# One limit and one power for the lengths of q and k, and the last group's attention mask applied after the exponential

## The chip, the cores and the metric

The kernel runs on one core of a Trainium2 chip. The time is what the device takes for one launch, in microseconds; of the kernel before there are three runs and one profiled execution.

The engines are called as in the profile: PE is TensorE (matrix products and transposes), PEld its loading of weights, DVE is VectorE, ACT is ScalarE, POOL is GpSimd, and SP is the engine whose queue issues most of the DMA transfers. L994 is line 994 of the kernel before.

## The reference

The input is 32 sequences of 256 tokens with 256 features in float32. First a recurrent block works on all of them: a projection to 512 channels and a gate, a causal convolution of four taps, a layer norm, a state of 16 x 512 that is updated and clipped token by token, and a projection back to 256. Then two transformer layers follow, and the input is added at the end. The change concerns the attention of these layers:

```python
h = shift_token(x)
q, k, v = jnp.split(h @ wqkv, 3, axis=-1)      # 8 heads of 64
q = l2norm(q) * qs                             # t / clip(norm(t), 1e-12), per token and head
k = l2norm(k) * ksc
q, k = rotary_xpos(q, k)
sim = jnp.einsum('bhwid,bhwjd->bhwij', bq * 8, bk)
mask = (i < j) | (i > j + WINDOW) | (j == -1)  # window of 128, causal
sim = jnp.where(mask, -finfo.max, sim)
out = jnp.einsum('bhwij,bhwjd->bhwid', softmax(sim), bv)
x = x + out @ wo
```

A query sees the keys of its own window of 128 tokens that are not later than itself, and those keys of the window before that lie at most 128 tokens back. With 256 tokens there are two windows. After the attention comes a feed-forward network with a gelu gate of width 682.

## The kernel before

**Stages.** The 32 sequences form four groups of 8. The recurrence (the scan) runs over a whole group at once, with 256 steps per group, and each step is one DVE instruction (L703) on a state of 128 x 512. Its results go to DRAM and are loaded again as the residual tiles for the layers. The layers then work on one sequence at a time. The order is group, layer, sequence: 4 x 2 x 8 = 64 passes, called sequences below. While the layers work on one group, the scan of the next groups is mixed in between; for the last group no scan is left, and its 16 passes run by themselves.

**Order.** The program is written as a pipeline by hand. Each of the 64 passes has 8 slots (`ST = 8`), and `stage(n, i, ...)` puts a piece of work into slot i of pass n. `attend` (L1393) places the attention's pieces: the scores in slots 2, 3 and 5, the row sums and the weighted values in slot 7, the division and the output projection in the slots of the next pass, and in the same slots the projections of the next pass's v (slots 0 and 3), q and k (slots 1 and 4), with the transposes of q and k in slots 6 (first window) and 8 (second window). `feed` (L1411) places the feed-forward network two passes later. A planner then orders the instructions of each engine, by the order in which they were written and by its own estimate of when their inputs are ready; `keep_in_program_order` pins an instruction behind what its engine was given before. [...]

**q and k.** `project_qkv` (L957) multiplies 128 tokens by the weights into a PSUM bank. `rotated` (L971) then does, for q and again for k: the squares on ACT (L975), the two products with the rotary tables on DVE (L978, L983), their sum on POOL (L986), the sum of squares per head on DVE (L988), a lower limit for it on DVE (L992), the power -1/2 on POOL (L994), and the multiplication of the rotated tile by it on POOL (L995). `turn` (L998) transposes the tile on PE and copies it by ACT.

**Scores and mask.** `scores` (L1153) makes scores with the keys as rows and the queries as columns, for one window of keys and a number of head pairs. It fills two PSUM banks of 128 x 512. In each bank the first matmul multiplies an identity by the mask, in bfloat16, and so writes 0 or -32768 (L1161); the matmuls of q and k add to it (L1168). The exponential on ACT (L1177) turns masked places into 0. A pass has three such calls, with two banks each: keys of window 1 (slot 2, `kw` = 1, four head pairs by 128 queries), and keys of window 0 for two head pairs by 256 queries at a time (slots 3 and 5). `sums` (L1181) and `values` (L1198) read the tiles pT from SBUF. There are 6 buffers for pT, one pass's worth, and 8 PSUM banks for everything.

A branch at the start takes an exact form of the program (`exact`, with a row maximum) where the scales of q and k are large; with these inputs it is not taken.

Of the kernel before, what the change touches and what calls it, by code (L numbers as in the profile page):

```python
# [19 lines left out]
P = 128  # L20
# [53 lines left out]
def kernel(  # L74
# [88 lines left out]
    for j in range(NJ):  # L163
# [23 lines left out]
        fill=MASKED_LOW, base=0, pattern=[[-1, W]], channel_multiplier=1,  # L187
    )

    head_cols = const.tile([P, 2, 32], FP, tag="head_cols", name="head_cols")  # L190
# [28 lines left out]
    def program(ctx, exact):  # L219
# [750 lines left out]

        def rotated(l, ps, w, a):  # L971


            sq = ap_.tile([P, DI], FP, tag="swp", name="sq", bufs=3)
            nc.scalar.activation(sq, ps, AF.Square)  # L975
            rot = ap_.tile([P, HEADS, DH], FP, tag="rot", name="rot", bufs=4)
            ph = ps.rearrange("p (h d) -> p h d", h=HEADS)
            nc.vector.tensor_mul(rot, ph, bc(rc_sb[:, l, w, a], 1, HEADS))  # L978
            swp = ap_.tile([P, HEADS, DH], FP, tag="swp", name="swp", bufs=3)
            hd = DH // 2  # L980
            for i in range(2):
                o, s = slice(i * hd, (i + 1) * hd), slice((1 - i) * hd, (2 - i) * hd)
                nc.vector.tensor_mul(  # L983
                    swp[:, :, o], ph[:, :, s], bc(rs_sb[:, l, w, a, o], 1, HEADS)
                )
            nc.gpsimd.tensor_add(rot, rot, swp)  # L986
            ss = aw.tile([P, HEADS], FP, tag="ss", name="ss")
            nc.vector.tensor_reduce(  # L988
                ss, sq.rearrange("p (h d) -> p h d", h=HEADS), AX.X, ALU.add
            )  # L990

            nc.vector.tensor_scalar_max(ss, ss, 1e-24)  # L992
            rn = aw.tile([P, HEADS], FP, tag="rn", name="rn")
            nc.gpsimd.tensor_tensor(rn, ss, neg_half, ALU.pow)  # L994
            nc.gpsimd.tensor_mul(rot, rot, bc(rn, 2, DH))  # L995
            return rot

# [37 lines left out]
        def attention(l):  # L1035

            for b in range(GB):

                qTs, kTs, vs = [], [], []
                for w in range(NW):  # L1040
                    for a in (2, 0, 1):
                        ps = project_qkv(b, w, a)
                        if a == 2:
# [3 lines left out]
                            continue  # L1047
                        rot = rotated(l, ps, w, a)
                        dst = ap_.tile(
# [77 lines left out]
        class Attention:  # L1127

            def __init__(self, l):
                self.l = l
                self.qkv, self.rot, self.p, self.o = {}, {}, {}, {}

            def project(self, b, w, a):
# [6 lines left out]
                if a == 2:  # L1142
                    nc.scalar.copy(self.qkv[b][2][:, w], ps)
                else:
                    self.rot[b, w, a] = rotated(self.l, ps, w, a)

# [6 lines left out]
            def scores(self, b, kw, i0, n):  # L1153
# [5 lines left out]
                for r in range(2):  # L1159
                    sc = ps_w.tile([P, n, nq], FP, tag="w", name="sc")  # L1160
                    nc.tensor.matmul(  # L1161
                        sc, ident_b, bc(mask_t[:, 0:nq], 1, n), start=True, stop=False
                    )
                    banks.append(sc)
                for i in range(n):
                    for r in range(2):
# [4 lines left out]
                            qT[rows, i0 + i, kw * W :],  # L1171
                            start=False,
                            stop=(i == n - 1),
                        )
                for r in range(2):
                    p = aw.tile([P, n, nq], FP, tag="pT", name="pT", bufs=6)
                    nc.scalar.activation(p, banks[r], AF.Exp)  # L1177
                    for i in range(n):
                        self.p[b, kw, i0 + i, r] = p[:, i, :]

            def sums(self, b):  # L1181
# [211 lines left out]
        def attend(n, at, b, nxt):  # L1393
# [3 lines left out]
            stage(n, 2, at.scores, b, 1, 0, HEADS // 2)  # L1397
            stage(n, 5, at.scores, b, 0, 2, 2)
            stage(n, 7, at.sums, b)
            stage(n, 7, at.values, b)  # L1400
# [33 lines left out]

        ats = [Attention(l) for _, l, _ in seqs]

# [157 lines left out]
```

## Time and profile before

| | |
|---|---|
| median of three runs | 3718.45 us |
| lowest and highest run | 3712.51 and 3718.55 us |
| profiled execution, its own time | 3716.42 us |
| its span, first to last instruction | 3714.5 us |
| TensorE clock granted, mean | 0.989 |
| attention's first instruction on POOL (L986) | 506.8 us |
| last step of the scan (L703) starts | 2876.3 us |
| mask matmuls (L1161) | 384 |
| limits (L992) and powers (L994) of q and k | 256 each |

The page gives busy times of the engines over the span, a strip of 40 slices, the chain of work that ended last, and groups of instructions by line. A group shows count, busy time in us, mean duration in ns of one, and after the second bar the time that the engine stood idle before instructions of this group, with the instruction that ended most of it. Matmuls overlap, so the duration of one is longer than the step to the next; the step is read from the chain, whose pieces follow each other in time.

### The profile page before, as it was taken

Reading aid. Unit: us, or ns where it says so; the run is one execution under the profiler, and the core shown is the slowest. Engines: PE = TensorE matmul, PEld = TensorE weight load, DVE = VectorE, ACT = ScalarE, POOL = GpSimd, SP = SyncE. Lnnn points to the kernel's source line nnn. Section 1 sums busy time; section 2 is a strip of 40 time slices with the busy share of each in tenths; the row PEclk is TensorE's granted clock in tenths of the full one; section 3 lists DMA queues with packets and bytes.
Section 4 is the critical chain, followed back from the end, with each engine's and each line's share of the span. In section 5 each row is a group of like instructions: output and inputs, shape, how many; then the busy total and the mean of one; then the engine's idle time right before and its main releaser. Section 6 shows DMA issues by size and latency. Waiting matters only on the chain.

```text
span 3714.5 us, 56989 instructions
## 1 busy us (share of the span) xinstructions
PE 3594.4 (97%) x19900; PEld 2240.4 (60%) x19900; DVE 2671.9 (72%) x5113; ACT 2161.5 (58%) x3689; POOL 1775.9 (48%) x1712
## 2 busy tenths in 40 slices
PE   7999889999999999999999999999999999999999
PEld 4444335666566566666666666666666666666666
DVE  5888889888787877887778777887776444444443
ACT  3666656666666666666666666666666444444442
POOL 4433366445455555554556555554444444433441
PEclk9999999999999999999999999999999999999999
DMA  7777655445454545445454546445453211011101
GB/s 205 203 198 203 185 164 149 130 110 135 121 140 122 150 129 150 125 112 133 110 138 124 140 138 148 126 108 137 106 135 98 60 35 50 12 35 33 30 27 36
DMA packets 469212, 435.79 MB, mean 117 GB/s; under 512 B 228835, under 2 KB 308532, under 8 KB 468788
## 3 DMA queue, kind: packets, MB, share of 16 engines
q1 hardware_dynamic: 384466, 420.05, 41.7%
q10 hardware_dynamic: 84450, 12.01, 2.1%
q8 instruction: 160, 2.62, 0.3%
q14 instruction: 136, 1.11, 0.1%
HBM read 383.70 MB, written 46.66 MB: 116 GB/s over the span
## 4 chain that ended last, share of the span: by engine, by line
PE 66%; DVE 15%; DMA 6%; POOL 5%; ACT 4%; issue 3%; SPq 0%; ACTq 0%; DVEq 0%; POOLq 0%
PE ps_qkv L962 13%; PE pa L1309 13%; PE po_f L1337 8%; DVE h L703 6%; PE y L715 5%; PE ps_wo L1012 4%; DMA xrep<-xnd 4%; PE sc L1168 4%; PE ov L1206 3%; PE ps_out L793 2%; PE ps_in L395 2%; PE tr_qk L1001 2%; ACT xrep L693 2%; DVE acc L485 2%; PE rs L1187 2%
## 5 line engine op out<-in xcount | busy, mean ns | idle before, releaser
L703 DVE CUSTOM_DVE_ANT_0 h<-h,xrep,lim 128x512 f32<-128x512 f32 x1024 | 950.2, 928 | 235.4 <-ACT xrep L693 200.8
L693 ACT ACTIVATE xrep<-xrep,beta 128x512 f32<-128x512 f32 x960 | 673.7, 719 | 342.5 <-DMA xrep<-xnd 252.5
L962 PE MATMUL ps_qkv<-qkv,res 128*128 128x512 f32 x1536 | 724.4, 607 | 18.4 <-DVE ag L1325 8.1
L1309 PE MATMUL pa<-hT,w 128*128 128x256 f32 (+1 forms) x3072 | 688.8, 386 | 1.4 <-ACT hT L1288 0.7
L1309 PEld LDWEIGHTS pa<-hT,w 128*128 128x128 f32 (+1 forms) x3072 | 492.7, 178 | 186.1 <-issue 77.4
L986 POOL TENSOR_TENSOR rot<-rot,swp 128x512 f32<-128x512 f32 x256 | 335.2, 1309 | 505.4 <-DVE swp L983 399.0
L962 PEld LDWEIGHTS ps_qkv<-qkv,res 128*128 128x128 f32 x1536 | 277.8, 191 | 327.9 <-issue 251.1
L994 POOL TENSOR_TENSOR rn<-ss,neg_half 128x8 f32<-128x8 f32 x256 | 459.2, 1794 | 15.2 <-DVE ss L992 5.2
L1325 DVE SCALAR_TENSOR_TENSOR ag<-pa,b_sb,ag 128x256 f32<-128x256 f32 (+1 forms) x448 | 213.4, 476 | 259.8 <-ACT ag L1317 257.3
L1337 PE MATMUL po_f<-ag,w 128*128 128x256 f32 (+1 forms) x1536 | 386.9, 393 | 11.6 <-DVE ag L1325 7.7
L715 PE MATMUL y<-h,ly 128*32 128x512 f32 x2048 | 356.5, 611 | 14.0 <-DVE h L703 13.1
L1337 PEld LDWEIGHTS po_f<-ag,w 128*128 128x128 f32 (+1 forms) x1536 | 272.7, 189 | 119.0 <-issue 52.0
L1262 POOL TENSOR_TENSOR rstd<-ve,neg_half 128x2 f32<-128x2 f32 x64 | 46.3, 723 | 622.3 <-DVE ve L1260 604.0
L995 POOL TENSOR_TENSOR rot<-rot,rn 128x512 f32<-128x512 f32 x256 | 292.4, 1142 | 20.1
L975 ACT ACTIVATE sq<-ps_qkv 128x512 f32<-128x512 f32 x256 | 151.9, 595 | 227.7 <-PE ps_qkv L962 175.7
L1317 ACT ACTIVATE ag<-pa,b_sb 128x256 f32<-128x256 f32 x320 | 150.2, 469 | 202.4 <-PE pa L1309 201.3
L978 DVE TENSOR_TENSOR rot<-ps_qkv,rc_sb 128x512 f32<-128x512 f32 x256 | 174.8, 683 | 82.9 <-ACT sq L975 82.2
L485 DVE SCALAR_TENSOR_TENSOR acc<-xr,wc_sb,acc 128x256 f32<-128x256 f32 x384 | 194.1, 529 | 53.7 <-POOL acc L474 53.2
L1012 PE MATMUL ps_wo<-oT,wo 128*128 128x256 f32 x1024 | 231.8, 379 | 0.2 <-ACT ag L1317 0.2
L1177 ACT ACTIVATE pT<-sc 128x512 f32<-128x512 f32 x384 | 208.5, 596 | 23.9 <-PE sc L1168 22.4
L1168 PE MATMUL sc<-qT,kT 64*128 64x128 f32 (+1 forms) x2048 | 222.0, 346 | 0.0
L1012 PEld LDWEIGHTS ps_wo<-oT,wo 128*128 128x128 f32 x1024 | 194.2, 190 | 28.3 <-ACT ag L1317 1.2
(150 smaller groups left out, 5437.0 us busy)
## 6 DMA issues: line engine op xcount, KB each, us to landing
xrep<-xnd SPq DMA_DIRECT2D x960, 256.0 KB
rb<-inv SPq DMA_DIRECT2D x128, 256.0 KB
xnd<-xn SPq DMA_DIRECT2D x64, 256.0 KB
qkv<-in_wqkv_dram SPq DMA_DIRECT2D x24, 512.0 KB
ahead<-xs_a SPq DMA_DIRECT2D x48, 256.0 KB
xp<-ahead SPq DMA_DIRECT2D x48, 256.0 KB
xd<-xnd SPq DMA_DIRECT2D x192, 64.0 KB
w<-in_w_dram SPq DMA_DIRECT2D x80, 128.0 KB
```

The costliest lines, as they stand in the source:

```text
L485: nc.vector.scalar_tensor_tensor(acc, xr[:, :, k : k + CH], wc_sb[:, ch, k : k + 1], acc, ALU.mult, ALU.add,)
L693: scaled = nc.scalar.activation(bx, ck[c].pop(("bx", t), bx), AF.Copy, scale=ck[c]["beta"][:, t : t + 1])
L703: nc.vector._custom_dve(TENSOR_ADD_SAT, out=h_new, in0=state["h"], in1=bx, s0=ck[c]["lim"][:, 0, t : t + 1], s1=ck[c]["lim"][:, 1, t : t + 1],
L715: nc.tensor.matmul(ck[c]["y", hb][32 * q : 32 * q + 32, :], ly[hb % 2][:, 32 * t : 32 * t + 32], ck[c].pop(("h", hb * TB + t)), start=(i = ...
L962: nc.tensor.matmul(ps, res[b][:, k, t0 : t0 + W], wt["qkv", a][:, k], start=(k == 0), stop=(k == KM - 1),)
L986: nc.gpsimd.tensor_add(rot, rot, swp)
L994: nc.gpsimd.tensor_tensor(rn, ss, neg_half, ALU.pow)
L995: nc.gpsimd.tensor_mul(rot, rot, bc(rn, 2, DH))
L1012: nc.tensor.matmul(po[:, d], wt["wo", 0][:, c, d * P : (d + 1) * P], oT[:, c, :], start=(c == 0), stop=(c == NC_ - 1),)
L1168: nc.tensor.matmul(banks[r][:, i, :], kT[rows, i0 + i, kw * W : (kw + 1) * W], qT[rows, i0 + i, kw * W :], start=False, stop=(i == n - 1),)
L1309: nc.tensor.matmul(pg if x else pa, wt["w1", m][:, k, x], self.h[:, k], start=(k == 0), stop=(k == KM - 1),)
L1337: nc.tensor.matmul(self.po[:, d], wt["w2", 0][r0 : r0 + n, m, d * P : (d + 1) * P], self.ag[m][r0 : r0 + n], start=(m == 0), stop=(m == le ...
```

## The change

The change has two parts.

First, the lengths of q and k of one window are kept in one tile of 128 x 2 x 8. `rotated` gets its half of it and ends with the sum of squares; a new function `normed` applies the limit and the power once to both halves (16 columns) and then multiplies the two rotated tiles. It is called after k, in the same slot in which k's rotation was before.

Second, the passes of the last group (`apart`) write no mask into PSUM. Every matmul of q and k there starts and stops its own accumulation. After the exponential, a new function `mask` multiplies the tile pT by a mask of ones and zeros in bfloat16, made once at the start on POOL. For the keys of window 1 this is done on POOL, in slot 3; for those of window 0 on DVE, in slots 4 and 6. Each of these multiplications is pinned behind what its engine was given before. The other three groups keep the mask matmul.

```diff
--- before.py
+++ after.py
@@ -186,6 +186,9 @@
         out=mask_t[:, W : 2 * W], in_=mask_t[:, W : 2 * W], compare_op=ALU.is_ge,
         fill=MASKED_LOW, base=0, pattern=[[-1, W]], channel_multiplier=1,
     )
+
+    mask_1 = const.tile([P, 2 * W], BF, tag="mask_1", name="mask_1")
+    nc.gpsimd.tensor_scalar(mask_1, mask_t, -1.0, None, ALU.is_ge)
 
     head_cols = const.tile([P, 2, 32], FP, tag="head_cols", name="head_cols")
     nc.gpsimd.memset(head_cols, 0.0)
@@ -968,7 +971,7 @@
                 )
             return ps
 
-        def rotated(l, ps, w, a):
+        def rotated(l, ps, w, a, ss):
 
 
             sq = ap_.tile([P, DI], FP, tag="swp", name="sq", bufs=3)
@@ -984,16 +987,22 @@
                     swp[:, :, o], ph[:, :, s], bc(rs_sb[:, l, w, a, o], 1, HEADS)
                 )
             nc.gpsimd.tensor_add(rot, rot, swp)
-            ss = aw.tile([P, HEADS], FP, tag="ss", name="ss")
             nc.vector.tensor_reduce(
                 ss, sq.rearrange("p (h d) -> p h d", h=HEADS), AX.X, ALU.add
             )
+            return rot
+
+        def lengths():
+            return aw.tile([P, 2, HEADS], FP, tag="ss", name="ss")
+
+        def normed(rots, ss):
+
 
             nc.vector.tensor_scalar_max(ss, ss, 1e-24)
-            rn = aw.tile([P, HEADS], FP, tag="rn", name="rn")
-            nc.gpsimd.tensor_tensor(rn, ss, neg_half, ALU.pow)
-            nc.gpsimd.tensor_mul(rot, rot, bc(rn, 2, DH))
-            return rot
+            rn = aw.tile([P, 2, HEADS], FP, tag="rn", name="rn")
+            nc.gpsimd.tensor_tensor(rn, ss, bc(neg_half, 1, 2), ALU.pow)
+            for a, rot in enumerate(rots):
+                nc.gpsimd.tensor_mul(rot, rot, bc(rn[:, a], 2, DH))
 
         def turn(rot, dst):
             tr = ps_w.tile([P, HEADS // 2, W], FP, tag="w", name="tr_qk")
@@ -1045,7 +1054,11 @@
                             nc.scalar.copy(v_sb, ps)
                             vs.append(v_sb)
                             continue
-                        rot = rotated(l, ps, w, a)
+                        if a == 0:
+                            rots, ss = [], lengths()
+                        rots.append(rotated(l, ps, w, a, ss[:, a]))
+                    normed(rots, ss)
+                    for a, rot in enumerate(rots):
                         dst = ap_.tile(
                             [P, HEADS // 2, W], FP, tag="kT1" if a else "qT1",
                             name="kT" if a else "qT", bufs=3 if a else 2,
@@ -1128,9 +1141,11 @@
 
 
 
-            def __init__(self, l):
+            def __init__(self, g, l):
                 self.l = l
-                self.qkv, self.rot, self.p, self.o = {}, {}, {}, {}
+
+                self.apart = g == NG - 1
+                self.qkv, self.rot, self.p, self.ps, self.o = {}, {}, {}, {}, {}
 
             def project(self, b, w, a):
                 if w == 0 and a == 2:
@@ -1142,7 +1157,11 @@
                 if a == 2:
                     nc.scalar.copy(self.qkv[b][2][:, w], ps)
                 else:
-                    self.rot[b, w, a] = rotated(self.l, ps, w, a)
+                    if a == 0:
+                        self.ss = lengths()
+                    self.rot[b, w, a] = rotated(self.l, ps, w, a, self.ss[:, a])
+                    if a == 1:
+                        normed([self.rot[b, w, i] for i in range(2)], self.ss)
 
             def turn(self, b, w):
                 for a in range(2):
@@ -1158,9 +1177,10 @@
                 banks = []
                 for r in range(2):
                     sc = ps_w.tile([P, n, nq], FP, tag="w", name="sc")
-                    nc.tensor.matmul(
-                        sc, ident_b, bc(mask_t[:, 0:nq], 1, n), start=True, stop=False
-                    )
+                    if not self.apart:
+                        nc.tensor.matmul(
+                            sc, ident_b, bc(mask_t[:, 0:nq], 1, n), start=True, stop=False
+                        )
                     banks.append(sc)
                 for i in range(n):
                     for r in range(2):
@@ -1169,14 +1189,25 @@
                             banks[r][:, i, :],
                             kT[rows, i0 + i, kw * W : (kw + 1) * W],
                             qT[rows, i0 + i, kw * W :],
-                            start=False,
-                            stop=(i == n - 1),
+                            start=self.apart,
+                            stop=self.apart or i == n - 1,
                         )
                 for r in range(2):
                     p = aw.tile([P, n, nq], FP, tag="pT", name="pT", bufs=6)
                     nc.scalar.activation(p, banks[r], AF.Exp)
+                    self.ps[kw, i0, r] = p
                     for i in range(n):
                         self.p[b, kw, i0 + i, r] = p[:, i, :]
+
+            def mask(self, kw, i0):
+
+                e = nc.gpsimd if kw else nc.vector
+                for r in range(2):
+                    p = self.ps.pop((kw, i0, r))
+                    n, nq = p.shape[1:]
+                    tc.keep_in_program_order(
+                        e.tensor_mul(p, p, bc(mask_1[:, 0:nq], 1, n))
+                    )
 
             def sums(self, b):
 
@@ -1396,6 +1427,9 @@
             stage(n, 3, at.scores, b, 0, 0, 2)
             stage(n, 2, at.scores, b, 1, 0, HEADS // 2)
             stage(n, 5, at.scores, b, 0, 2, 2)
+            if at.apart:
+                for i, what in ((3, (1, 0)), (4, (0, 0)), (6, (0, 2))):
+                    stage(n, i, at.mask, *what)
             stage(n, 7, at.sums, b)
             stage(n, 7, at.values, b)
             stage(n + 1, 0, at.put_inverse)
@@ -1432,7 +1466,7 @@
             if l == L - 1 and g < NG - 1:
                 stage(n + 6, 2, load_res, g + 1, b)
 
-        ats = [Attention(l) for _, l, _ in seqs]
+        ats = [Attention(g, l) for g, l, _ in seqs]
 
         for n, (g, l, b) in enumerate(seqs):
             nxt = (ats[n + 1], seqs[n + 1][2]) if n + 1 < len(seqs) else None
```

## The prediction

> **What bounds the kernel now.** I read the page first, for the share of each engine and its course over the 40 slices.
>
> ```profile
> span 3714.5 us, 56989 instructions
> PE 3594.4 (97%) x19900; PEld 2240.4 (60%) x19900; DVE 2671.9 (72%) x5113; ACT 2161.5 (58%) x3689; POOL 1775.9 (48%) x1712
> PE   7999889999999999999999999999999999999999
> DVE  5888889888787877887778777887776444444443
> POOL 4433366445455555554556555554444444433441
> ```
>
> TensorE is nearly full throughout. From about slice 31 on DVE halves: the recurrence has ended there (its last step starts at 2876.3), and only attention and feed-forward are left. A mean over both stretches says little, so next I took the busy times by stretch: scan before attention is in full flow, scan beside attention, the change between, and the last group's attention.
>
> ```profile
> 500.00:1000.00 500.00, 475.08 (x2671) 286.28 (x2670) 422.50 (x790) 314.01 (x547) 279.11 (x265) 0.98 0.50 131
> 1000.00:2876.00 1876.00, 1850.71 (x10720) 1173.22 (x10720) 1480.25 (x2789) 1188.91 (x2027) 970.17 (x904) 1.00 0.48 128
> 2990.00:3715.00 725.00, 716.55 (x4116) 486.97 (x4114) 310.17 (x658) 317.93 (x502) 276.81 (x218) 1.00 0.12 32
> ```
>
> Columns: length, then PE, PEld, DVE, ACT and POOL busy, clock, DMA share, GB/s. In the last stretch PE lacks 8.4 us in all, most of it the final 7 us after its last matmul; DVE has 415 us free and POOL 448. Beside the scan PE is idle for 25 + 25 = 50 us in 2376.
>
> Third, the chain of waits inside the last group, over the second half of one sequence:
>
> ```profile
> 3219.86 3.63 PE ps_qkv L962 x8
> 3223.49 0.43 PE sc L1161 x2
> 3223.92 1.09 PE sc L1168 x16
> 3225.02 2.98 PE po_f L1337 x12
> 3228.00 0.59 PE tp_hn L1282 x4
> 3228.58 0.43 PE sc L1161 x2
> 3229.01 1.06 PE sc L1168 x8
> ```
>
> Each piece starts when the one before it ends, and all are PE's. L1161 is the mask's matmul pair: 0.43 us on the path each time. The pieces recur with a period of 41.6 us, one sequence each (the same L962 piece starts at 2938.78, 2980.39 and 3022.01). Fourth, the operations of the change, grouped by shape:
>
> ```profile
> L994 POOL TENSOR_TENSOR rn<-ss,neg_half 128x8 f32<-128x8 f32 x256 | 459.2, 1794 | 15.2 <-DVE ss L992 5.2
> L992 DVE TENSOR_SCALAR ss<-ss 128x8 f32<-128x8 f32 x256 | 118.8, 464 | 0.6
> L1161 PE MATMUL sc<-mask_t,ident_b 128*128 128x512 bf16 x384 | 116.2, 381 | 5.6 <-DVE ag L1325 4.5 <-DVE zT L784 1.2
> L1230 DVE TENSOR_TENSOR oT<-oT,rb 128x1024 f32<-128x1024 f32 x64 | 79.9, 1249 | 0.0
> ```
>
> The 381 ns of L1161 is one instruction from start to end, overlapped with its neighbours; what it costs PE is its 0.43/2 = 0.215 us step in the chain. Busy time and step differ, and the step is what a removal returns.
>
> [...] medians 568 ns on one column (L552), 703 on two (L1262), 1647 on eight (L994). [...]
>
> **The change, part by part.**
>
> *Masks leave PE.* Three score calls with two banks each drop 6 mask matmuls per sequence, 16 sequences: 96 x 0.215 = 20.7 us. All 96 lie behind 2990, where the chain is PE without a gap, so this comes off in full. With the mask goes its load of ident_b (98 ns, under running matmuls); the first kT load (188 ns) must now hide under what precedes, 512-column projections or 128-column transposes. If it shows behind the transposes, that costs at most 0.1 us x 16 = 1.6. I take 0. The scores' own start and stop flags change no column count: 0.
>
> *Masks on POOL and DVE.* Per sequence POOL gets 2 multiplies of 128x512. Nearest row: rot plus swp L986, median 1272 ns, so 2.5 us; DVE gets 4 at 0.69, so 2.8 us. Over 16 sequences 41 us and 44 us, into 448 and 415 us of free time. Lateness decides, not load. The values need the last pair of masks: in the last full sequence the exponentials of that pair end at 3619.3, DVE is free then until its next ag product at about 3621, and the sums start on PE at 3625.8. That leaves 6.5 us for 1.4 us of masking, 5.1 spare. The POOL pair follows scores whose exponentials end at 3601.1, waits for the rotation chain running until 3606.6, ends near 3609.1, and has over 16 us left. In the last sequence, with no projections beside it, the figures are 3650.5 and 3656.1: 5.6 us for 1.4. Behind the masks in the queues stand fo's addition on POOL (starts 3610.0 now) and the ag products on DVE; a late mask would hold the first, which only feeds a store, and the second, which PE needs some 10 us later (L1337 at 3635.8). Cost: 0; if the cover were gone, 1.4 us x 16 = 22 us, the whole gain.
>
> *One limit for q and k.* 128 instructions of 464 ns leave DVE, 59 us; the one left has 16 columns instead of 8, which adds next to nothing: the one-column form (L551) has 148 ns and the eight-column form 149 at least. In the scan beside attention (92 of the 128 pairs) that is 43 us of 1903 busy.
>
> *One power.* No row has 16 columns. From 2 to 8 columns the slope is (1647-703)/6 = 157 ns, giving 1647 + 8 x 157 = 2.90 us for 16, against 3.29 for two: 0.39 us less per pair, 50 us less POOL time. Bounds: if only the first 8 columns cost, 1.65 (1.65 saved per pair)[...]. I take 2.90.
>
> *Order.* On POOL, add, power, multiply twice over become two adds, one power, two multiplies. The q rotation is ready later by k's arrival, and k's at about the same time as now. Who waits is the transpose L1001, which past 1000 us starts 7.8 us or more after the multiply that it needs; only in the first sequence, before 530, three of them wait, 6.1 us of PE's 50 idle. What else is late beside the scan: DVE's ag, rhs, h and fo, some 37 us. With DVE 2.3% and POOL about 3% lighter, these waits shrink somewhat: between 0 and all 50. If a queue's wait goes as load over free time, DVE going from 0.80 to 0.783 takes a tenth, 5 us; in proportion to load alone, 1. I take 3. In the last group this part is worth 0, as PE doesn't wait there.
>
> *Setup.* One POOL operation on mask_t, 0.3 to 0.7 us, falls into POOL's 1.08 us wait for the limit's comparison at 3.6 to 4.7: 0.
>
> **Sum.** 20.7 + 3 = 23.7 off the profiled execution's own time of 3716.4 (its span 3714.5 and 1.9 around it): 3692.7. The median of the runs is 2.0 above that execution, which would put it at 3694.8; the runs reach from 3712.5 to 3718.6, so I keep 3693.
>
> **Rivals.**
>
> *The scan gains more.* DVE is 79 to 84% busy beside the scan, and shares of its work stand in the chain (DVE 15% of the whole span, POOL 5%). If half of PE's 50 us idle goes: 20.7 + 25 off, 3671; with a smaller part, up to 3684. Against it: PE is 98.7% busy from 1000 on, so only some 25 us are there to be had, and not all of those follow DVE.
>
> *The masks take the place of the matmuls.* The sums wait for DVE or POOL as they never waited for a mask before. From 5.1 us of lateness on PE loses time, at 6.4 the sequence has lost its 1.29 us. Times from 3705 to 3716. For it: masks are pinned behind what their engine was given before, and POOL's chain is long. Against it: DVE's stretch after 3619.3 is empty.
>
> *Slower: the longer POOL block holds the scan.* The two adds, the power and the multiplies occupy POOL for about 7.5 us with a power of 2.9 in the middle, and the scan's own small POOL steps (L552, L474, L656) stand behind it[...]. In the chain such a place exists: power, multiply, power, multiply, L587, L474 in a row near 1590 to 1600. If each of 92 pairs holds the scan's step by up to the extra 1.25 us, and PE has no other work, the loss is up to 115 us; it decides from 28/92 = 0.31 us per pair, where the 20.7 are eaten and 7.4 lost. At half a microsecond each: 3716.4 - 20.7 + 46 = 3742; I put it at 3735. A new placement of the instructions by the planner would show as this too. Against it: PE idle is only 25 us after 1000.
>
> That the change doesn't happen is excluded for the masks: whether a sequence is of the last group is fixed when the program is built, and 16 of 64 are.
>
> **How the numbers follow.** The forecast 0.62, its own range 3684 to 3702 (power, scan 0 to 10, and runs 3 us apart); the scan's larger gain 0.12; masks exposed 0.12; slower 0.14. Two in ten outside: the upper end at 3716 leaves out the slower case, the lower at 3676 leaves out half of the larger gain. No change within 0.2% is 7.4 us, about what a measurement of this kernel can tell: faster means below 3711. Faster 0.62 + 0.12 + 0.04 (masks half exposed) = 0.78, same 0.08, slower 0.14.
>
> **What would show it.** L1161 at x288; the last group's period at 41.6 - 1.29 = 40.3 us, with PE still without gaps; 128 powers near 2.9 us and 128 limits; 32 mask multiplies on POOL near 1.27 and 64 on DVE near 0.69; last scan step near 2873. I am wrong if sums L1187 show waits for masks, if the period stays above 41, or if the last scan step moves by more than 10 us either way.

## The result and the profile after

| | before | after |
|---|---|---|
| median | 3718.45 us | 3700.07 us |
| lowest and highest of 5 runs | 3712.51 and 3721.18 | 3698.57 and 3707.73 |
| profiled execution, its own time | 3716.42 us | 3698.57 us |

The ratio of after to before is 0.9959, with an interval of 0.9946 to 0.9973: faster by 0.41%, or 15.2 us of 3718 (10 to 20).

To see where this came from I cut each trace at the divisions of the attention, one DVE product per sequence (L1230 before, L1261 after), and read their starts from the timeline. The **start** runs to the first division, the **scan** from the 1st to the 45th (attention beside the recurrence), the **last stretch** from the 45th to the 64th (all 16 sequences of the last group lie in it).

| us | start | scan | last stretch |
|---|---|---|---|
| before | 584.9 | 2313.5 | 772.4 |
| after | 576.8 | 2324.8 | 751.6 |
| difference | -8.1 | +11.3 | -20.8 |

The last stretch gained what the masks promised. The scan, where a gain of 3 us was forecast, lost 11.3. Of the 8.1 us of the start, 7.6 are there when the first projection of q begins (492.1 against 499.7 us), and of the change only the one operation for the mask runs before that. I take them for chance: two kernels with the same work up to the first division reach it 8 us apart (after and the kernel with late masks, 576.8 and 585.0). The scan repeats better: three kernels with the same work there (after, late masks, lengths alone) gave 2324.8, 2323.8 and 2324.0.

The scan has a quieter part. Ahead of the 13th division the two traces show TensorE's granted clock at half now and then, 24 us in all before and 17 after from the 1st on, and runs of one kernel differ in the mean clock (0.986 to 0.990 in the five of after). From the 13th to the 45th the mean clock is 1.00 in both, and these 32 sequences took 1667.3 us before (1231.1 to 2898.4) and 1677.7 after (1223.9 to 2901.6). So 10.4 of the 11.3 us are lost there, 0.3 us per sequence.

The page of after, first the totals and then three strips of 40 slices:

```profile
span 3696.8 us, 56674 instructions
PE 3576.4 (97%) x19804; PEld 2228.2 (60%) x19804; DVE 2688.6 (73%) x5049; ACT 2161.6 (58%) x3689; POOL 1742.8 (47%) x1617
PE   7999988999999999999999999999999999999999
DVE  6888888878777777887787777877776445555553
POOL 4433456445445554544455545444443444443451
```

TensorE has lost 18 us of busy time, and the course over the slices is as before. The busy times by stretch (length, then PE, PEld, DVE, ACT, POOL, clock, DMA share, GB/s):

```profile
500.00:1000.00 500.00, 473.82 (x2684) 285.96 (x2681) 409.14 (x774) 314.93 (x547) 265.80 (x248) 0.98 0.50 129
1000.00:2876.00 1876.00, 1842.85 (x10659) 1167.62 (x10660) 1444.34 (x2702) 1181.34 (x2016) 919.94 (x825) 1.00 0.48 128
2990.00:3697.00 707.00, 698.94 (x4027) 479.85 (x4026) 373.18 (x692) 318.95 (x504) 303.98 (x221) 1.00 0.13 34
```

In the second line DVE is busy for 36 us less than before and POOL for 50 less, and yet PE's idle time went up, from 25.3 us to 33.2. In the third, the chain of waits is still PE's alone, and the mask's pieces of 0.43 us are gone from between the others:

```profile
3216.59 3.63 PE ps_qkv L965 x8
3220.22 1.09 PE sc L1188 x16
3221.31 2.98 PE po_f L1368 x12
3224.29 0.59 PE tp_hn L1313 x4
3224.88 1.06 PE sc L1188 x8
```

The period is now 40.32 us (the row sums L1218 start at 3206.38 and 3246.70). The groups that the change touched, and below them DVE's second products before, which are L986 after:

```profile
L1003 POOL TENSOR_TENSOR rn<-ss,neg_half 128x16 f32<-128x16 f32 x128 | 376.2, 2939 | 54.4 <-DVE ss L1001 48.2 <-DVE stat L561 0.7
L1001 DVE TENSOR_SCALAR ss<-ss 128x16 f32<-128x16 f32 x128 | 42.6, 333 | 0.6
L1181 PE MATMUL sc<-mask_t,ident_b 128*128 128x512 bf16 x288 | 87.7, 380 | 7.8 <-DVE ag L1356 7.5
L986 DVE TENSOR_TENSOR swp<-ps_qkv,rs_sb 128x256 f32<-128x256 f32 x512 | 191.4, 415 | 31.0 <-POOL rot L989 30.9
```

```profile
L983 DVE TENSOR_TENSOR swp<-ps_qkv,rs_sb 128x256 f32<-128x256 f32 x512 | 191.5, 415 | 1.8 <-POOL rot L986 1.2
```

Behind the second bar two waits have grown. POOL stood idle for 54.4 us ahead of the power (15.2 before), 48.2 of it for the one limit. DVE stood idle for 31.0 us ahead of the products L986 (1.8 before). The mask multiplications, minimum, median and maximum in ns:

```profile
L1209 DVE TENSOR_TENSOR pT<-pT,mask x64: 676/679/1753, 3031.0 to 3638.1; 128x512 f32<-128x512 f32 x64
L1209 POOL TENSOR_TENSOR pT<-pT,mask x32: 1152/1154/1160, 3027.7 to 3621.7; 128x512 f32<-128x512 f32 x32
```

### The profile page after: what moved, and what is told of

Its sections match the earlier page's. It is cut to its first block, busy times and chain, and to the rows that moved or that the text cites. A ratio compares the mean times of both kernels' runs of the same rounds, so it can differ in the third digit from the quotient of the medians.

```text
span 3696.8 us, 56674 instructions
## 1 busy us (share of the span) xinstructions
PE 3576.4 (97%) x19804; PEld 2228.2 (60%) x19804; DVE 2688.6 (73%) x5049; ACT 2161.6 (58%) x3689; POOL 1742.8 (47%) x1617
## 4 chain that ended last, share of the span: by engine, by line
PE 69%; DVE 13%; DMA 5%; POOL 5%; ACT 4%; issue 3%; ACTq 0%; DVEq 0%; SPq 0%; POOLq 0%
PE ps_qkv L965 14%; PE pa L1340 14%; PE po_f L1368 8%; DVE h L706 6%; PE ps_wo L1021 5%; PE y L718 5%; PE sc L1188 4%; DMA xrep<-xnd 4%; PE ov L1237 3%; PE ps_out L796 3%; PE tr_qk L1010 2%; PE ps_in L398 2%; DVE acc L488 2%; PE rs L1218 2%; ACT xrep L696 2%
## 5 line engine op out<-in xcount | busy, mean ns | idle before, releaser
L706 DVE CUSTOM_DVE_ANT_0 h<-h,xrep,lim 128x512 f32<-128x512 f32 x1024 | 961.7, 939 | 237.7 <-ACT xrep L696 200.5
L965 PE MATMUL ps_qkv<-qkv,res 128*128 128x512 f32 x1536 | 724.3, 607 | 20.8 <-DVE ag L1356 9.5
L989 POOL TENSOR_TENSOR rot<-rot,swp 128x512 f32<-128x512 f32 x256 | 325.1, 1272 | 565.8 <-DVE swp L986 451.3
L1003 POOL TENSOR_TENSOR rn<-ss,neg_half 128x16 f32<-128x16 f32 x128 | 376.2, 2939 | 54.4 <-DVE ss L1001 48.2
L978 ACT ACTIVATE sq<-ps_qkv 128x512 f32<-128x512 f32 x256 | 151.9, 595 | 225.1 <-PE ps_qkv L965 165.4
L1197 ACT ACTIVATE pT<-sc 128x512 f32<-128x512 f32 x384 | 208.4, 596 | 18.2 <-PE sc L1188 16.2
L986 DVE TENSOR_TENSOR swp<-ps_qkv,rs_sb 128x256 f32<-128x256 f32 x512 | 191.4, 415 | 31.0 <-POOL rot L989 30.9
```

The source lines that it names most:

```text
L706: nc.vector._custom_dve(TENSOR_ADD_SAT, out=h_new, in0=state["h"], in1=bx, s0=ck[c]["lim"][:, 0, t : t + 1], s1=ck[c]["lim"][:, 1, t : t + 1],
L965: nc.tensor.matmul(ps, res[b][:, k, t0 : t0 + W], wt["qkv", a][:, k], start=(k == 0), stop=(k == KM - 1),)
L1003: nc.gpsimd.tensor_tensor(rn, ss, bc(neg_half, 1, 2), ALU.pow)
```

## The experiments

The theory on record: the masks give 20.7 us in the last group, and the lengths hardly matter for the time. Its main rival after the result: the lengths cost some 10 us beside the scan and hide a part of the masks' gain. All kernels here compute the whole of the reference. Each ratio is to the kernel before on the same chip, so ratios compare across rows and medians don't. The scan and the last stretch are cut as above; "13th on" is the part of the scan from the 13th to the 45th division. Times of stretches are of one trace each; rows with the same work differ by up to 2.3 us in the scan and 1.9 in this part.

| kernel | median us | ratio, interval | scan us | 13th on us | last stretch us |
|---|---|---|---|---|---|
| before | 3718.45 | 1 | 2313.5 | 1667.3 | 772.4 |
| after | 3700.07 | 0.9959, 0.9946 to 0.9973 | 2324.8 | 1677.7 | 751.6 |
| masks alone | 3693.33 | 0.9947, 0.9930 to 0.9964 | 2311.2 | 1666.5 | 751.6 |
| lengths alone | 3723.91 | 1.0027, 1.0020 to 1.0035 | 2324.0 | 1678.7 | 772.4 |
| after, masks late | 3729.30 | 1.0036, 1.0025 to 1.0047 | 2323.8 | 1676.8 | 778.8 |
| lengths alone, two powers | 3728.87 | 1.0043, 1.0029 to 1.0057 | 2332.8 | 1680.3 | 772.4 |
| lengths alone, two limits and powers | 3722.15 | 1.0015, 1.0006 to 1.0024 | 2316.8 | 1671.8 | 772.4 |
| lengths alone, named buffers | 3704.42 | 0.9980, 0.9973 to 0.9987 | 2314.1 | 1666.6 | 772.4 |
| masks alone, named buffers | 3678.48 | 0.9902, 0.9887 to 0.9918 | 2304.8 | 1663.7 | 751.6 |
| after, sum first | 3672.89 | 0.9882, 0.9861 to 0.9902 | 2305.6 | 1655.7 | 751.9 |
| masks alone, sum first | 3663.86 | 0.9866, 0.9851 to 0.9882 | 2289.6 | 1650.8 | 751.6 |
| after, sum first, named buffers | 3674.80 | 0.9893, 0.9879 to 0.9908 | 2307.6 | 1657.8 | 751.6 |
| masks alone, sum first, named buffers | 3662.08 | 0.9858, 0.9843 to 0.9873 | 2289.4 | 1649.3 | 751.6 |
| after, window-1 masks on POOL throughout | 3723.75 | 1.0032, 1.0020 to 1.0045 | 2352.3 | 1699.7 | 750.7 |

### Each part alone

The masks alone: after, with `rotated` as before (limit, power and multiplication at its end, for q and for k).

> Only the last group's masks leave TensorE; q and k keep a limit and a power each. If the two parts add up and the masks' part is 20.7 us: about 3697 us median, 0.9944 of before, the stretch from the division of the 45th sequence to that of the 64th shorter by 20.5 to 21 us (772.4 before, 751.6 in the changed kernel), and the scan as in the kernel before. If the merged lengths are what cost time beside the scan, this kernel is faster than the changed one, by 3 us or more; if the merged lengths give time, slower.

The lengths alone, against after:

```diff
-    mask_1 = const.tile([P, 2 * W], BF, tag="mask_1", name="mask_1")
-    nc.gpsimd.tensor_scalar(mask_1, mask_t, -1.0, None, ALU.is_ge)
...
-                self.apart = g == NG - 1
+                self.apart = False
```

> Only the lengths of q and k are taken together; all masks stay on TensorE. As forecast: 3 us faster than before (0 to 10). If the changed kernel's trace tells the truth about the steady part of the scan, where it lost some 11 us between the 1st and the 45th sequence: 0 to 10 us slower than before, with 128 powers near 2.91 us, vector waits of some 30 us for the sum on GpSimd ahead of the second rotary product, and the last group as in the kernel before (772 us from the 45th to the 64th division). If that loss is only a fluctuation between executions: no difference from before beyond 3 us.

The masks alone take 20.8 us off the last stretch and leave the scan within 2.3 us of before: 0.53% faster, about 20 us. The lengths alone leave the last stretch as it was and add 10.5 us to the scan: 0.27% slower, 10 us. The two parts add up to a gain of 10 us by the ratios; after shows 15.2. The intervals reach 6 us to either side for the masks, 3 for the lengths and 5 for after, so the sum and the whole agree within them. The change is a gain with a loss inside.

### The cover of the masks

All three masks go into slot 7, where the row sums are.

```diff
-                for i, what in ((3, (1, 0)), (4, (0, 0)), (6, (0, 2))):
+                for i, what in ((7, (1, 0)), (7, (0, 0)), (7, (0, 2))):
```

> The changed kernel with all six mask multiplications of a sequence put into slot 7, directly ahead of the row sums that read them, so that nothing covers them. If the cover is what makes the masks free: TensorE waits for them in each of the 16 sequences; four multiplications of 0.68 on the vector engine in a row, after the scores have long been there, give up to 2.7 us per sequence, 20 to 45 us in all, and the last group takes back the whole gain (3715 to 3740 us). If they are off the path wherever they are put, because other matmuls lie between in the planner's order: within 3 us of the changed kernel.

The last stretch takes 778.8 us, 27.2 more than in after, or 1.7 per sequence: all of the masks' gain and 6 us beyond. The waits of that kernel in the last group (engine and line that wait, releaser: us in total, times, longest):

```profile
PE rs L1218 <- DVE pT L1209: 12.4, 22, 0.9
PE rs L1218 <- POOL pT L1209: 2.1, 8, 0.7
```

The weight loads of the sums wait for masks for another 28.1 us. In after no matmul of the sums waits for a mask; only weight loads do, for 2.7 us in all. So the masks are free in after because of where they stand. The price without cover, forecast as 22 us, is 27.2 with all three late.

### What in the lengths costs

Three kernels undo the merging by steps, all without the masks' part. In the first the power is two of 8 columns again, after the one limit:

```diff
-            nc.gpsimd.tensor_tensor(rn, ss, bc(neg_half, 1, 2), ALU.pow)
+            for i in range(2):
+                nc.gpsimd.tensor_tensor(rn[:, i], ss[:, i], neg_half, ALU.pow)
```

> The limit merged, the powers of q and k separate (two of 8 columns, one after the other after the limit), all masks on TensorE. GpSimd has 0.38 us more per pair than with one power, 35 us beside the scan. If the length of the GpSimd block is what costs time: 2328 to 2340 us from the 1st to the 45th division, slower than with one power (2324.0). If the block's length is hidden and the loss is the place where both lengths now end, after k: within 2 us of 2324.0. If the single long power holds up the scan's small steps: faster, 2313 to 2320.

In the second the limits are two again as well, so that its instructions are those of before, and only their place is after k:

```diff
-            nc.vector.tensor_scalar_max(ss, ss, 1e-24)
...
-            nc.gpsimd.tensor_tensor(rn, ss, bc(neg_half, 1, 2), ALU.pow)
             for a, rot in enumerate(rots):
+                nc.vector.tensor_scalar_max(ss[:, a], ss[:, a], 1e-24)
+                nc.gpsimd.tensor_tensor(rn[:, a], ss[:, a], neg_half, ALU.pow)
```

> The lengths of before with nothing merged: two limits of 8 columns and two powers of 8 columns, only placed after the rotation of k; masks as before. If the place of q's length after k is what the merged form costs: 2328 to 2342 us from the 1st to the 45th division (2313.5 before, 2332.8 with one limit and two powers), and DVE's waits for POOL's acc and stat at least 50 and 35 us. If the one limit of 16 columns is itself what costs: 2311 to 2318 us, and those waits near before's 38.7 and 27.6 us.

This expectation joined a time and a set of waits, and they came apart: the time is that of the second answer (2316.8 us), the waits are those of the first. DVE's waits between 580 and 2880, before:

```profile
DVE acc L485 <- POOL acc L474: 38.7, 70, 3.2
DVE stat L558 <- POOL stat L552: 27.6, 18, 1.8
```

With two limits and two powers after k:

```profile
DVE acc L486 <- POOL acc L475: 55.0, 69, 5.2
DVE stat L559 <- POOL stat L553: 41.1, 20, 2.7
```

These two waits grew by 30 us together, and the scan by only 3.3 (4.5 from the 13th division on). With the lengths alone they grew by 18 and the scan by 10.5. That DVE waits longer for the scan's small POOL steps thus can't be most of what costs; I had read it as the cause until this run.

The steps between the four kernels give a better account:

| us | scan | of it, 13th on |
|---|---|---|
| from before to the place after k | +3.3 | +4.5 |
| from two limits to one | +16.0 | +8.5 |
| from two powers to one | -8.8 | -1.6 |
| together | +10.5 | +11.4 |

The one limit is the largest step in both columns. Some 7 us each of the second step and of the third lie ahead of the 13th division, where the granted clock was 0.98 before and 0.99 after, not 1.00 (over the whole profiled execution it was 0.988 with two limits, 0.986 with one limit and two powers, and 0.986 with one of each); how much of the 7 us belongs to the powers isn't known. Timed runs agree in order, 1.0015, 1.0043 and 1.0027; the first two intervals are apart, those of the last step overlap. In the last step no instruction moved: these two kernels have them in the same order on every engine but for the power itself. In the step before, other instructions moved with the limit, on DVE 41 of some 4,900, and about 15 each on ACT and POOL.

What one limit does is seen in the timeline of DVE, lengths alone (start, duration, instruction), around one pair:

```profile
2071.37 0.76 DVE L984 TENSOR_TENSOR swp<-ps_qkv,rs_sb 128x256 f32<-128x256 f32 x2 [0.26 <-POOL rot L987]
2072.04 0.68 DVE L988 TENSOR_REDUCE ss<-sq 128x8 f32<-128x512 f32 x1
2072.63 1.39 DVE L704 CUSTOM_DVE_ANT_0 h<-h,xrep,lim 128x512 f32<-128x512 f32 x1
2073.94 0.16 DVE L999 TENSOR_SCALAR ss<-ss 128x16 f32<-128x16 f32 x1
```

and in that of POOL:

```profile
2072.20 1.27 POOL L987 TENSOR_TENSOR rot<-rot,swp 128x512 f32<-128x512 f32 x1 [0.51 <-DVE swp L984]
2074.18 2.91 POOL L1001 TENSOR_TENSOR rn<-ss,neg_half 128x16 f32<-128x16 f32 x1 [0.71 <-DVE ss L999]
```

The limit needs k's sum of squares, and behind that sum DVE has a scan step of 1.39 us. POOL is done with k's addition at 2073.47 and stands for 0.71 us, although q's sum has been there since 2070.5. With two limits q's power follows the additions at once:

```profile
2063.02 1.27 POOL L987 TENSOR_TENSOR rot<-rot,swp 128x512 f32<-128x512 f32 x1 [0.50 <-DVE swp L984]
2064.39 2.14 POOL L1002 TENSOR_TENSOR rn<-ss,neg_half 128x8 f32<-128x8 f32 x1
```

and k's limit runs under it. The wait recurs at 64 pairs. POOL's wait for the limit between 580 and 2880, before and with lengths alone:

```profile
POOL rn L994 <- DVE ss L992: 4.4, 7, 1.2
```

```profile
POOL rn L1001 <- DVE ss L999: 45.3, 64, 0.7
```

It is 45.4 us with two powers, and no such wait is listed with two limits. So 45 us of POOL's waiting come with the one limit, and 8 to 16 us of the whole. That the one brings about the other isn't shown (see the buffers below). How the loss reaches PE is spread out: PE's waits in 1000 to 2850 are mostly for DVE's `ag` product, 20.3 us in all before, 24.7 with two limits, 27.8 with one limit and two powers, 24.7 with lengths alone. No single wait carries the loss, and I leave the path to PE open.

### Why fewer DVE instructions gave no time: sum of squares first

Before, the limits took 464 ns at the mean and 149 at least. The timeline of before shows what the rest was; DVE's limit, and POOL's addition for q beside it:

```profile
2062.13 0.33 DVE L992 TENSOR_SCALAR ss<-ss 128x8 f32<-128x8 f32 x1
```

```profile
2061.16 1.27 POOL L986 TENSOR_TENSOR rot<-rot,swp 128x512 f32<-128x512 f32 x1 [4.89 <-PE tp_hn L1282]
```

The limit ends at 2062.46, POOL's addition at 2062.43. Another limit, at 2079.93 and 1.00 us long, ends at 2080.93 with an addition that ends at 2080.90. Both end 0.03 us after the addition, and so it is with all the long ones: of the 256 limits, 176 took longer than 200 ns, and each of these ended 25 to 33 ns after an instruction of POOL; the 29 that began while POOL ran nothing took 167 ns at most. So taking q's limit away took from DVE, in good part, not work but a place to wait in. What stood behind it, k's products, now waits for the same addition: the 0.26 us before L984 above, 17.9 us over 580 to 2880 (1.2 before).

To test this I moved the sum of squares ahead of the products with the tables, so that the limit can run before POOL's addition begins. In after, and in masks alone:

```diff
+            nc.vector.tensor_reduce(
+                ss, sq.rearrange("p (h d) -> p h d", h=HEADS), AX.X, ALU.add
+            )
             nc.vector.tensor_mul(rot, ph, ...)
...
-            nc.vector.tensor_reduce(
-                ss, sq.rearrange("p (h d) -> p h d", h=HEADS), AX.X, ALU.add
-            )
```

> The changed kernel with the sum of squares (vector reduction) put ahead of the rotary products instead of behind them; same work otherwise. The buffer that k's second product takes is then q's squares, which the reduction has freed, and not q's product, for which GpSimd's sum is waited for. If that wait (31 us of idle vector time in the changed kernel) holds up the scan: 3 to 12 us faster than the changed kernel, some 3690 us. If it is time that nobody needed: within 3 us of the changed kernel, with the wait below 5 us all the same. If the placement by the planner decides alone: a shift of up to 10 us either way, with no relation to the wait.

> A limit and a power for each of q and k as in the kernel before, the last group's masks off TensorE, and the sum of squares ahead of the rotary products. If the early sum of squares is good by itself: about as fast as the kernel with merged lengths and the early sum (2305.6 us from the 1st to the 45th division), within 4 us, some 3675. If only the merged lengths under that order gain, because the limits then are fewer: 5 us or more slower than it, up to the 2311 us of the masks alone.

Both gained more than either answer on record allowed for.

The groups of the limit, masks alone, and the same with the sum first:

```profile
L995 DVE TENSOR_SCALAR ss<-ss 128x8 f32<-128x8 f32 x256 | 117.8, 460 | 0.6
```

```profile
L995 DVE TENSOR_SCALAR ss<-ss 128x8 f32<-128x8 f32 x256 | 43.5, 170 | 0.0
```

The same 256 instructions take 74 us less, and the scan 21.6 us less (2311.2 to 2289.6). This order is worth more than the whole change, with lengths apart. With lengths together it brings 19.2 (2324.8 to 2305.6). POOL no longer waits for the limit there, nor DVE ahead of `swp`; but together is still 16.0 us behind apart in the scan, 4.9 of them from the 13th division on. So these two waits can't account for the loss here, and what costs wasn't found. One thing differs: the one power took 3.16 us at the mean here, 2.94 in after, while the two apart took 1.77 each with the sum first and 1.79 without.

The two stretches leave the start out, and the ratios don't. With the sum first and lengths together, the first sequence, from its first projection of q to its division, took 78 us in both kernels, against 82 and 86 with lengths apart. By the ratios together is therefore less far behind: 6 us, with intervals that overlap, and 13, with intervals apart, with the named buffers of the next part.

### The buffers

The other suspect was the three buffers that `sq`, `swp` and others share in turn, since DVE now waited ahead of `swp`. Three named buffers, so that `swp` of k takes the one of `sq` of q:

```diff
-            sq = ap_.tile([P, DI], FP, tag="swp", name="sq", bufs=3)
+            sq = ap_.tile([P, DI], FP, tag="swC" if a else "swA", name="sq", bufs=1)
...
-            swp = ap_.tile([P, HEADS, DH], FP, tag="swp", name="swp", bufs=3)
+            swp = ap_.tile([P, HEADS, DH], FP, tag="swA" if a else "swB", name="swp", bufs=1)
```

The other tiles of this tag are given to the three as well.

> The lengths taken together, all masks on TensorE, the order of the instructions in the source as in the changed kernel, but the three buffers for squares and second products given out by name: k's second product takes the buffer of q's squares, so it waits for no sum on GpSimd. If the 31 us of that wait are what makes the merged lengths 11 us slower: 2310 to 2315 us from the 1st to the 45th division, against 2324.0 with the lengths merged and 2313.5 before. If they are idle time that would have passed otherwise: 2321 to 2327, with the wait gone all the same.

The scan is back at 2314.1 us, DVE's wait ahead of `swp` is gone, and this run alone would have closed the case. No instruction moved between it and the lengths alone. The control is the same edit where the lengths are apart:

> The last group's masks off TensorE, a limit and a power for each of q and k, and the three buffers given out by name, so that k's second product needs no sum on GpSimd. In the kernel before that product came right behind q's limit, and the limit in turn ended as GpSimd's sum for q ended (at 2062.46 and 2062.43 us in one place), so the limit held the vector engine as long as the buffer would have. If so, freeing the buffer gains nothing while the limit is there: 2309 to 2314 us from the 1st to the 45th division (2311.2 for the masks alone), and the limits keep a mean near 0.46 us. If the buffer held it: 2300 to 2306.

There it brings 6.4 us too, the second answer on record, though the masks alone had next to no such wait. With lengths together it brings 9.9; by the ratios it is some 17 us in both. Over the whole scan, then, some 3 us of it belong to what the change did, and together stays 9.3 us behind apart. From the 13th division on, where the clock doesn't blur it (1.00 between 1000 and 2850 in all four kernels), the picture is another: 12.1 us with lengths together, 2.8 with lengths apart, and together is 2.9 behind.

There the suspect is not cleared. POOL's wait for the limit stood in full in the kernel with named buffers (45.3 us), and most of the loss was gone. In the kernel with two limits after k it was the other way round: no wait for the limit, DVE's wait ahead of `swp` as with one (18.2 us between 580 and 2880), and 4.5 us lost. With either wait alone the loss is 3 to 5 us from the 13th division on, with both 11 to 13. This is a reading of single traces, and it names no single cause. The last two runs join the buffers with the sum first:

> As the run with separate lengths and the early sum of squares, with the three buffers given out by name as well. There the second product waited for no sum on GpSimd before (no idle time ahead of it), so 2287 to 2292 us from the 1st to the 45th division as without it (2289.6); outside of that, the naming of the buffers does something else, as at the start, where the setup's tiles use them too.

> The changed kernel with the early sum of squares and the buffers given out by name. With the early sum alone 2305.6 us from the 1st to the 45th division, 16 more than with separate lengths under the same order. If the merged lengths cost that by what GpSimd does late (the scan's own steps behind the block of two sums, one power and two products), the buffers change nothing: 2302 to 2308. If it is still the buffers: near 2290.

With the sum first the buffers do nothing: 2289.4 against 2289.6 apart, 2307.6 against 2305.6 together. In all four arrangements lengths together lose to lengths apart: by 10.5, 9.3, 16.0 and 18.2 us in the scan, and by 11.4, 2.9, 4.9 and 8.5 from the 13th division on.

### More masks off TensorE

In after with the sum first, the masks for keys of window 1 also go to POOL in the other three groups.

```diff
-                    if not self.apart:
+                    if not (self.apart or kw):
...
+            stage(n, 3, at.mask, 1, 0)
```

> The changed kernel with the sum of squares first, and in all four groups the mask for the keys of window 1 on GpSimd (two multiplications of 1.15 us per sequence), so two of six mask matmuls leave TensorE beside the scan too. If TensorE sets the pace there as in the last group: 0.43 us less for each of some 45 sequences, 19 us, 3650 to 3657. If GpSimd's extra 2.3 us per sequence delay the scan's steps: no gain or a loss, 3670 to 3700.

The scan grew by 46.7 us over its parent (2352.3 against 2305.6), more than either answer on record. PE's largest wait there is for DVE:

```profile
PE sc L1181 <- DVE ag L1356: 44.1, 13, 4.0
```

It was 9.6 us in the parent. That isn't all of the loss. The granted clock was 0.978 to 0.981 in its six runs and 0.988 to 0.992 in the parent's four. In the profiled executions it was 0.979 over 3721.5 us and 0.988 over 3674.9, and by an estimate from these four numbers some 34 us more of full clock are missing. A removal that pays in full in the last group costs in the scan: PE waits longer for DVE's products, and less clock was granted. How the masks on POOL make these products late, and whether the waits and the clock belong together, wasn't followed.

## Why the prediction was right or wrong, point by point

- **Masks leave PE**: right. 20.8 us for 20.7 (96 times 0.215 is 20.6), 751.6 us in six kernels alike; the step from the chain was the right price, the 380 ns of one instruction would not have been.
- **Masks on POOL and DVE**: cost nothing, as forecast; 1154 ns for 1272 on POOL, 679 at the median for 0.69 us on DVE. No row was shown for the 0.69; before has one, the product of the same shape L978 (128x512), with 681 at the median. At the mean DVE's took 875 and 54 us in all, not 44; that lay in free time. The weight loads' 2.7 us lie under running matmuls: PE's only listed wait in the last group is 0.6 us, for `fo`.
- **First kT load**: it waits once in the last group, 0.4 us. Right.
- **One limit**: the size was right and the conclusion wrong. The group shrank by 76 us, forecast 59, and DVE is 36 us less busy beside the scan, forecast 43. But part of those 464 ns was waiting for POOL, and it came back as the 30.9 us ahead of `swp`. The kernel with two limits after k, where nothing was saved, has this wait too.
- **One power**: 2.91 us at the median, 2.94 at the mean, for 2.90. The saving was undersized: I took medians, and at their means two powers of 1.79 make way for one of 2.94, 0.65 us per pair and 83 us of POOL in all, not 50. It is the one part of the lengths that gains, 8.8 us in the scan of one trace and 1.6 from the 13th division on.
- **Order**: here it failed. I named the transpose as the only one that waits for q, and looked for slack there. I didn't ask what POOL itself would do between the last addition and the power. It waits for k's sum and a scan step on DVE, 0.71 us at 64 pairs; and DVE waits for POOL's addition ahead of k's second product. The gain of 3 us became a loss of 10.5 to 11.3, and the range of 0 to 10 had the wrong sign. "DVE and POOL are lighter, so waits shrink" was a sum over load, and waits grew where the order of the queues had changed. The four DVE waits that it put at 37 us make 32 between 500 and 2876.
- **Setup**: the operation took 866 ns, longer than the 0.3 to 0.7 taken, which was the author's estimate (before, POOL's three operations on `mask_t` took 0.29 to 0.31 us each). The start varies by more than that from trace to trace, so its effect can't be told.
- **Sum**: 23.7 us forecast, 17.9 in the profile, made of -20.8, +11.3 and the -8.1 of the start; by the ratio 15.2. The median is inside the likeliest case's range of 3684 to 3702, near its upper end. The profile's total came as near as it did by luck: without the shorter start, which no part of the change accounts for, the two stretches give 9.5 us.
- **Rivals**: the scan gained nothing, and no mask was exposed. The third had the right sign for the scan and the right engine, but the loss is 0.11 to 0.12 us per pair (10.5 or 11.3 over 92) where 0.31 decides. Its mechanism, POOL holding the scan's own steps, is real as a wait and costs little: with two limits it stands there in full and the scan is 3.3 us longer, 4.5 from the 13th division on.
- **What would show it**: the last scan step, at 2879.5, moved by 3.2 us, within the 10 that I allowed. That marker counted from the beginning of the launch, so the early start hid the scan's 11.3. It should have been measured from the scan's own beginning.

## What to carry to other kernels

When two short chains are merged, ask for every engine what the joint step now waits for and what stands in the queue ahead of that; instructions saved are no gain if an engine stands still for the later half (POOL for 0.71 us at 64 pairs here). A small instruction that is longer than its own minimum (464 ns at the mean here, 149 at least) may be waiting for another engine: removing it moved the wait here, to the 30.9 us ahead of `swp`, while reordering so that it ran clear of that engine removed it (170 ns at the mean, and 21.6 us of the scan, with nothing computed differently). And a fix that restores the time needs its control on the kernel without the fault, in a stretch that repeats: over the whole scan the named buffers gained 6.4 us where the wait was not and 9.9 where it was, and from the 13th division on 2.8 and 12.1.

The best version is the masks with lengths apart and the sum of squares first: 0.9866 (0.9851 to 0.9882), or 0.9858 (0.9843 to 0.9873) with named buffers, about 50 us below before, where after is 15 below.

## What was not expected of the hardware

- A DVE limit on 128x8 took 149 ns at least and up to 1259 beside POOL; every one above 200 ns (176 of 256) ended 25 to 33 ns after an instruction of POOL.
- A power of -1/2 on 16 columns took 2.91 us at the median, on the straight line through 703 ns for two columns and 1647 for eight (L1262 and L994 before), so that the broadcast exponent added nothing that can be seen. With the sum first it took 3.16 us at the mean, with and without named buffers, for 2.94 in after.
- Masking 128x512 on POOL by a bfloat16 mask took 1154 ns in the last group, with a spread of 8, where adding two float32 tiles took 1272 at the median.
- With the window-1 masks on POOL in all groups the granted clock was 0.978 to 0.981 in six runs, where the four of its parent had 0.988 to 0.992.
